# Attention with a quantised FFN on one core: v projected for two groups of heads at a time, and the start and the end of the kernel rearranged

## The chip, the cores and the metric

The kernel runs on one core of one Trainium2 chip. The core has engines that run side by side, each with its own queue of instructions in program order: PE (matrix products; PEld is its loading of the stationary operand), DVE (vector work), ACT (activation functions and copies), POOL (elementwise work) and SP (which here only starts DMAs). POOL and ACT can start DMAs too, from the same queues as their other work. The metric is the time on the device in microseconds (us); smaller is better.

## The reference

For x of shape (2, 1024, 512), with float32 data:

```python
def attn(x, w_q, w_k, w_v, w_o):                 # 32 heads of 16
    q, k, v = (proj(w) for w in (w_q, w_k, w_v)) # (2, 32, 1024, 16)
    scores = einsum('bhqd,bhkd->bhqk', q, k) / sqrt(16)
    out = einsum('bhqk,bhkd->bhqd', softmax(scores), v)
    return einsum('bse,oe->bso', merge_heads(out), w_o)

def bitlinear(x, w, scale):                      # ternary weights
    w_mean = mean(abs(w))
    return einsum('...i,oi->...o', x, clip(round(w / (w_mean + EPS)), -1, 1) * w_mean * scale)

def ffn(x, w_gate, w_up, w_down, ...):           # 512 -> 1376 -> 512
    xq = int4_quant(x)       # beta = mean|x| per token, values -8 to 7
    gate = square(relu(bitlinear(xq, w_gate, s_gate)))
    inter = int8_quant(bitlinear(xq, w_up, s_up) * gate)   # gamma = max|.| per token
    return bitlinear(inter, w_down, s_down)

x = x + attn(layernorm(x), ...)
x = x + ffn(layernorm(x), ...)
```

## The kernel before, in words

**Steps and slots.** The 32 heads are four groups g of eight; a group's heads lie in two sets s of four, 32 rows of the array each. The attention runs in 32 steps (batch b, half of the queries h, group g, set s), a step in 8 slots, one for each 128 keys. The loop over T runs the slots. In a slot PE forms scores for the exponentials (pse, line 515) and the scores of the next step for the row maxima (psm, line 475); ACT takes the exponentials (e, line 519), DVE the maxima (pm, line 485); PE then multiplies e with v (pso, line 545). The maxima are turned into rows by a small product (psn, line 498) and an ACT copy (mrow, line 502). All products of the attention are float32.

**Fillers.** Everything else is a generator whose pieces are laid between those products by the class `Fillers` while the program is built. It holds four lists: "proj", "norm", "ffn" and "back" (work without PE). A task may have a due slot; with fewer than `URGENT` (16) slots to go it comes first. A slot has a budget of PE time (`SHARE` or `MORE`). `WIDTH` says how many tasks of a list are looked at. A task that needs a PSUM bank yields ("take",), and ("give",) when done: it is given bank "o", or, if that is held, one of the score banks "s" if `fill.scores` allows (one in most of the loop's ends, three after the loop). `ensure(names)` runs fillers until the named tasks are done; it stands ahead of the loads of k (`load_k`, eight slots a step, five before the step) and of v (`load_v`, at slot 8n + 8). After the loop `turn()` goes through the tasks, one step of each in turn. The order of instructions on every engine is thus fixed when the program is built.

**The start.** `norm_inputs` loads four tiles of x by SP's queue (`xs`, line 280, four buffers), takes mean and variance on DVE, an inverse root by three Newton steps, normalises on DVE (line 294), transposes on PE (psx, line 302) and copies to xnT on ACT (line 303). Half 0 of the first batch runs straight away, then the first projections of k and q (psk and psq, line 390, `first_qk`); half 1, the rest of k and q for the first two steps and v of the first group are fillers. ACT's first instruction is the loading of its function table.

**Projections.** `project_qk` (lines 338 to 373) forms 128 x 512 of q or k in PSUM (line 351), copies it to `full` on ACT (line 359), casts to a rounded part `hi` and subtracts to get `lo` on POOL (lines 360, 361), and writes both to device memory by SP; `hi` and `lo` have two buffers each, `full` one. `project_v` (lines 410 to 437) runs for each (b, g, half): a 256 KB piece of weights wv by SP (line 333), 16 products of 128 x 128 by 128 columns into one bank (psv, line 418), two ACT copies into the one tile `vst` (line 430), which also holds columns of ones whose products give the softmax's sums, and two writes of 256 KB to vD by POOL's queue (line 432). `load_v` reads one (b, g, s) of 512 KB.

**Weights of the FFN.** A "back" task `weight_sums` (lines 627 to 646) loads 35 pieces of the three matrices by POOL's queue (tag raw, four buffers, three loads ahead) and sums absolute values on ACT (Abs into junk, line 640). Later `weight_quant` (lines 666 to 683) loads them again (raws), compares on POOL into `low` (line 677, two buffers) and makes the ternary fp8 weights on DVE.

**The end.** Work on the last step's sums: `normalise_last` copies the sums on ACT (den, line 589) and divides 128 columns (one tile of tokens) at a time, five DVE instructions each (lines 592 to 597, the result is OT). `output_proj` multiplies with w_o (psy, line 714; one product for each group, so four for a tile) and adds x on DVE (line 725), then statistics of the second normalisation (bn, root, beta; the sum of deviations `dev` on ACT). The last 512 tokens go in two calls of two tiles, (0, 1) and (2, 3). For each tile `ffn_input` normalises, clips and rounds (xn, xq, lines 768 to 774), transposes (psxq, line 780) and copies (xqT, ACT); `ffn_product` forms gate (pg) and up (pu) in three pieces of 512, 512 and 352 columns (line 801), with two ACT instructions on each gate piece (lines 811, 813) and on DVE the product of both (inter, line 823); `ffn_output` takes the maximum (gm, line 841), a few steps of one column (lines 843 to 847), scales (v, line 850), rounds on ACT (iq, line 853), transposes by eight and three products (psiq, line 863) with ACT copies (iqT), multiplies by the down weights in eleven products (py, line 880), adds (y, line 887) and writes out. Where a generator yields ("gap", n), it rests for n turns, and what other tasks issue meanwhile stands in between.

## Time and profile before

| what | value |
|---|---|
| median of 3 runs | 1307.87 us (1304.2 to 1317.62) |
| the profiled execution's own time | 1320.16 us |
| its span, first to last instruction | 1318.4 us |
| mean granted clock of PE | 0.965 |
| PE busy | 1209.3 us, 92% |
| DVE, ACT, POOL busy | 866.5, 712.1, 246.5 us |
| chain that ended last | PE 74%, DVE 11%, ACT 5%, issue 4%, DMA 4% |

The profile is one execution. Busy times add up over instructions; a clock of 1.00 is full speed of PE, 0.50 half of it. The chain that ended last goes back from the last instruction to whatever released it, step by step. A row of waits reads: engine, product and line, what it waited for, then the total of us, the number of times and the longest.

### The profile page before, as it was taken

The numbers are of one execution on the slowest core, as the hardware profiler recorded it, in microseconds if no ns is written. First come the engines' busy times: TensorE is split into PE (matmuls) and PEld (weight loads), VectorE is DVE, ScalarE is ACT, GpSimd is POOL, SyncE is SP. The second block draws the span as 40 slices with busy tenths as digits, with TensorE's granted clock in tenths as the row PEclk, the third lists the DMA queues.
The fourth block names the chain that finished last, engine by engine and source line by source line (L and its number), as shares of the span: only waits on it lengthen the run. The fifth ranks groups of instructions, "written<-read, shape, count | busy, mean of one in ns | idle before, by whom it ended". The sixth has DMA issues, their size and how long they took to land.

```text
span 1318.4 us, 22143 instructions
## 1 busy us (share of the span) xinstructions
PE 1209.3 (92%) x9082; PEld 541.6 (41%) x9082; DVE 866.5 (66%) x1203; ACT 712.1 (54%) x903; POOL 246.5 (19%) x279
## 2 busy tenths in 40 slices
PE   5768899999999999999999999999999999999566
PEld 2345444334445443444444444444433344443222
DVE  6521468778865667687776676877776867772634
ACT  1124655545655555665666556666665556666243
POOL 1034326455511100321101003110010111100000
PEclk9889999999999999999999999999999979999769
DMA  3056666555333431221213223211133110201000
GB/s 112 0 184 216 225 199 214 156 177 191 126 107 122 136 110 58 89 81 58 72 47 106 95 76 117 76 55 67 57 107 95 58 57 34 82 26 33 24 0 33
DMA packets 72334, 127.88 MB, mean 97 GB/s; under 512 B 9680, under 2 KB 30160, under 8 KB 72232
## 3 DMA queue, kind: packets, MB, share of 16 engines
q1 hardware_dynamic: 64360, 101.16, 23.8%
q0 software_dynamic: 7872, 25.30, 5.9%
q8 instruction: 71, 1.16, 0.4%
q14 instruction: 31, 0.25, 0.1%
HBM read 89.25 MB, written 37.19 MB: 96 GB/s over the span
## 4 chain that ended last, share of the span: by engine, by line
PE 74%; DVE 11%; ACT 5%; issue 4%; DMA 4%; POOL 2%; SPq 0%; ACTq 0%; DVEq 0%; POOLq 0%
PE pse L515 22%; PE pso L545 16%; PE psm L475 8%; PE psy L714 5%; PE psv L418 4%; DVE pm L485 4%; PE psq L351 3%; PE pu L801 3%; PE py L880 3%; PE psk L351 3%; DMA wv<-in_wvT 2%; PE pg L801 2%; ACT e L519 2%; PE psn L498 1%; PE psk L390 1%
## 5 line engine op out<-in xcount | busy, mean ns | idle before, releaser
L485 DVE TENSOR_REDUCE pm<-psm 128x2 f32<-128x1024 f32 x512 | 621.5, 1220 | 336.9 <-PE pse L515 236.8
L519 ACT ACTIVATE e<-pse 128x1024 f32<-128x1024 f32 x512 | 523.0, 1024 | 415.3 <-PE pse L515 315.4
L475 PE MATMUL psm<-kst,qst 32*128 32x512 f32 x2048 | 372.8, 448 | 13.4 <-ACT e L519 8.2
L515 PE MATMUL pse<-qst,kst 32*128 32x512 f32 x2048 | 371.7, 446 | 10.2 <-DVE pm L485 8.8
L515 PEld LDWEIGHTS pse<-qst,kst 32*128 32x128 f32 x2048 | 151.5, 185 | 325.0 <-issue 160.6
L545 PE MATMUL pso<-e,v 128*32 128x512 f32 x2048 | 277.5, 612 | 0.7 <-ACT po L554 0.4
L515 PE MATMUL pse<-mrow,onesr 2*128 2x512 f32 x1024 | 208.6, 406 | 0.0
L475 PEld LDWEIGHTS psm<-kst,qst 32*128 32x128 f32 x2048 | 152.5, 186 | 39.1 <-ACT e L519 27.9
L515 PEld LDWEIGHTS pse<-mrow,onesr 2*128 2x128 f32 x1024 | 95.3, 185 | 5.1 <-ACT mrow L502 0.2
L815 POOL TENSOR_TENSOR g<-g 128x512 f32<-128x512 f32 (+1 forms) x36 | 34.2, 951 | 315.6 <-ACT g L811 315.6
L418 PE MATMUL psv<-wv,xnT 128*128 128x128 f32 x512 | 70.7, 294 | 14.2 <-DMA wv<-in_wvT 12.0
L545 PEld LDWEIGHTS pso<-e,v 128*32 128x32 f32 x2048 | 40.7, 108 | 97.4 <-issue 94.5
L418 PEld LDWEIGHTS psv<-wv,xnT 128*128 128x128 f32 x512 | 64.0, 203 | 27.3 <-issue 19.7
L714 PE MATMUL psy<-wo,OT 128*128 128x512 f32 x128 | 66.7, 635 | 5.9 <-DVE OT L597 5.9
L351 PE MATMUL psq<-xnT,wq 128*128 128x512 f32 x120 | 60.9, 622 | 1.4 <-ACT full_k L359 1.4
L351 PE MATMUL psk<-xnT,wk 128*128 128x512 f32 x112 | 58.4, 640 | 1.5 <-ACT vst L430 1.5
L677 POOL TENSOR_SCALAR low<-raws,whalf 128x512 bf16<-128x512 f32 (+2 forms) x35 | 52.8, 1510 | 21.4 <-DMA raws<-in_wuT 8.5
L801 PEld LDWEIGHTS <-xqT 128*128 128x128 bf16 x384 | 33.1, 102 | 57.5 <-issue 38.0
L770 POOL TENSOR_SCALAR xn<-x,mv,a 128x512 f32<-128x512 f32 x12 | 24.9, 2073 | 166.8 <-DVE a L747 166.7
L801 PE MATMUL pg<-wg,xqT 128*128 128x512 fp8e4 (+1 forms) x192 | 49.9, 387 | 4.0 <-DVE inter L823 2.4
L801 PE MATMUL pu<-wu,xqT 128*128 128x512 fp8e4 (+1 forms) x192 | 47.6, 372 | 3.5 <-ACT g L811 2.5
L880 PE MATMUL py<-wd,iqT 128*128 128x512 fp8e4 (+1 forms) x176 | 45.1, 392 | 2.9 <-ACT g L811 1.7
(124 smaller groups left out, 841.6 us busy)
## 6 DMA issues: line engine op xcount, KB each, us to landing
v<-vD SPq DMA_DIRECT2D x32, 512.0 KB
kst<-kD SPq DMA_DIRECT2D x30, 512.0 KB
qst<-qD SPq DMA_DIRECT2D x60, 256.0 KB
vD<-vst POOLq DMA_DIRECT2D x32, 256.0 KB, 5.4
qD<-hi_q SPq DMA_DIRECT2D x30, 256.0 KB
qD<-lo_q SPq DMA_DIRECT2D x30, 256.0 KB
x<-in_x SPq DMA_DIRECT2D x16, 256.0 KB
wq<-in_wqT SPq DMA_DIRECT2D x16, 256.0 KB
```

The costliest lines, as they stand in the source:

```text
L351: nc.tensor.matmul(ps, w[:, c, :], xnT[b, h][:, c, :], start=(c == 0), stop=(c == KC - 1))
L418: nc.tensor.matmul(ps[:, i * P : (i + 1) * P], xnT[b, half][:, c, i * P : (i + 1) * P], w[:, c, :], start=(c == 0), stop=(c == KC - 1),)
L475: nc.tensor.matmul(ps[:, r % 2, :], qst[n][l][rows, t * P : (t + 1) * P], kst[n][rows, kh * QB : (kh + 1) * QB], start=(l == 0), stop=(l = ...
L485: nc.vector.tensor_reduce(pm[n][:, t, kh, 2 * j : 2 * j + 2], ps, AX.X, ALU.max, negate=True)
L515: nc.tensor.matmul(ps[:, r % 2, :], left, right, start=(l == 0), stop=(l == 2))
L519: nc.scalar.activation(e, ps, AF.Exp, scale=SCALE)
L545: nc.tensor.matmul(acc[n][32 * r : 32 * r + 32, :], vt[n][:, i, r, :], e[r // 2][:, r % 2, :], start=(i == 0), stop=(i == NT - 1),)
L677: nc.gpsimd.tensor_scalar(low, w, h[:rows, m, 1:2], None, ALU.is_lt)
L714: nc.tensor.matmul(ps, OT[b, h, g][:, i * P : (i + 1) * P], wo[g], start=(g == 0), stop=(g == NG - 1),)
L801: nc.tensor.matmul(ps, xT[:, c, :], w[:, c, n : n + size], start=(c == 0), stop=(c == KC - 1))
L815: nc.gpsimd.tensor_tensor(g2[j], g2[j], g2[j], ALU.mult)
L880: nc.tensor.matmul(py, iqT[:rows, c, :], wd[:rows, c, :], start=(c == 0), stop=(c == FC - 1))
```

## The change

v is projected for two groups at a time: one 512 KB piece of weights for an even g and the next (tag "wv", one buffer, held over both halves), products of 256 columns, in two pieces k of eight products for each half, and a single `vst` for the piece, which four ACT copies fill and one DMA of 512 KB writes. There are tasks for even g only; the second half follows the first. `load_v` reads its part of the pair's vD. In `project_qk` the tile `full` goes: ACT copies into `lo`, from which POOL casts `hi` and subtracts in place. Raw pieces have three buffers and two loads ahead, `low` one buffer. At the start the odd tiles of x are loaded by ACT's queue, and two of the four copies of the first half are made by DVE. `ensure` runs only projections that are due no later than the named ones, and `WIDTH` for them is 7 until first_1 is done. At the end `normalise_last` is a "back" task that divides tiles 2 and 3 after the first call of `output_proj` is done, with a mark for each tile; the second call comes after the first; POOL makes xn for tiles 1 to 3; `ffn_output` for the last 512 tokens has no gaps between its DVE steps, and cd comes after v. `feed` takes up tasks that still wait for an "out" or "quant" task.

```diff
...
         self.now = self.slot = 0
+        self.WIDTH = dict(self.WIDTH)
...
             self.held.append((task["kind"], self.now + 1))
+            task["kind"] = ""
...
         start = self.now
+        tasks = [t for t in self.tasks["proj"] if t["name"] in names]
+        due = max((t["due"] for t in tasks), default=0)
         while not set(names) <= self.done:
-            self.run(1e9)
+            self._back()
+            task = 1
+            while task:
+                task = next(
+                    (t for t in self._candidates() if (t["due"] <= due and t["list"] == "proj" or t["kind"]) and self._ready(t)),
+                    None,
+                )
+                if task:
+                    self._step(task)
+            self.now += 1
...
     mcols = [const.tile([P, TQ, P], F32R, name=f"mcols{k}") for k in range(2)]
-    vst = [const.tile([P, 2, 4, 4, 32], F32, name=f"vst{k}") for k in range(1)]
+    vst = const.tile([P, 2, 2, 2, 4, 32], F32, name="vst")
     for m in mcols:
         nc.gpsimd.memset(m.bitcast(F32), 0.0)
-    for v in vst:
+    for g in range(2):
         for s in range(2):
-            nc.gpsimd.memset(v[:, s, :, :, 16 * (1 - s) : 16 * (1 - s) + 16], 1.0)
+            nc.gpsimd.memset(vst[:, g, s, :, :, 16 * (1 - s) : 16 * (1 - s) + 16], 1.0)
...
             xs[t] = sb.tile([P, H], F32, tag="x", name=f"x_{b}_{t}", bufs=4)
-            nc.sync.dma_start(xs[t], x[b, t * P : (t + 1) * P, :])
+            (nc.scalar if fast and t % 2 else nc.sync).dma_start(xs[t], x[b, t * P : (t + 1) * P, :])
...
                 nc.tensor.transpose(ps[:, c * P : (c + 1) * P], xs[t][:, c * P : (c + 1) * P], ident)
-            nc.scalar.copy(
-                xnT[b, half][:, :, i * P : (i + 1) * P], ps.rearrange("p (c t) -> p c t", c=KC)
-            )
+            dst = xnT[b, half][:, :, i * P : (i + 1) * P]
+            if fast and half == 0 and i % 2:
+                nc.vector.tensor_copy(dst, ps.rearrange("p (c t) -> p c t", c=KC))
+            else:
+                nc.scalar.copy(dst, ps.rearrange("p (c t) -> p c t", c=KC))
...
     vD = {
-        (b, g, s): dram.tile([P, NT, P], F32, name=f"vD_{b}_{g}_{s}")
-        for b in range(B)
-        for g in range(NG)
-        for s in range(2)
+        (b, g): dram.tile([4, P, NT * P], F32, name=f"vD_{b}_{g}") for b in range(B) for g in range(0, NG, 2)
...
         hi = sb.tile([P, QB], F32R, tag="hi", name=f"hi_{name}", bufs=2)
-        lo = sb.tile([P, QB], F32R, tag="lo", name=f"lo_{name}", bufs=2)
-        full = sb.tile([P, QB], F32, tag="full", name=f"full_{name}", bufs=1)
-        nc.scalar.copy(full, ps)
-        nc.gpsimd.tensor_copy(hi, full)
-        nc.gpsimd.tensor_tensor(lo, full, hi.bitcast(F32), ALU.subtract)
+        lo = sb.tile([P, QB], F32, tag="lo", name=f"lo_{name}", bufs=2)
+        nc.scalar.copy(lo, ps)
+        nc.gpsimd.tensor_copy(hi, lo)
+        nc.gpsimd.tensor_tensor(lo, lo, hi.bitcast(F32), ALU.subtract)
...
-        for l, part in enumerate((hi, lo)):
+        for l, part in enumerate((hi.bitcast(F32), lo)):
...
-                    nc.sync.dma_start(dst[a], part.bitcast(F32))
+                    nc.sync.dma_start(dst[a], part)
             else:
                 dst = kD[b, g].rearrange("(e l d) q -> l e d q", l=2, d=16)[l]
-                nc.sync.dma_start(dst[:, :, h * QB : (h + 1) * QB], part.bitcast(F32))
+                nc.sync.dma_start(dst[:, :, h * QB : (h + 1) * QB], part)
...
     def project_v(b, g, half, have):
-        w = proj_weights(wvT, g, f"wv_{b}_{g}_{half}")
-        yield ("gap", 4)
+        if half:
+            w = wt.pop((b, g, "v"))
+        else:
+            w = wt[b, g, "v"] = sb.tile([P, KC, 2 * P], F32, tag="wv", name=f"wv_{b}_{g}")
+            nc.sync.dma_start(
+                w, wvT.rearrange("(c p) e -> p c e", p=P)[:, :, g * P : (g + 2) * P]
+            )
+            yield ("gap", 4)
         yield from done(have)
-        yield ("take",)
-        ps = spare(f"psv_{b}_{g}_{half}")
-        for i in range(4):
-            for c in range(KC):
-                nc.tensor.matmul(
-                    ps[:, i * P : (i + 1) * P],
-                    xnT[b, half][:, c, i * P : (i + 1) * P],
-                    w[:, c, :],
-                    start=(c == 0),
-                    stop=(c == KC - 1),
-                )
-            if i < 3:
-                yield ("pe", 940.0)
-        v = vst[0]
-        src = ps.rearrange("p (t r s d) -> p t r s d", t=4, r=4, s=2)
-        for s in range(2):
-            nc.scalar.copy(v[:, s, :, :, 16 * s : 16 * s + 16], src[:, :, :, s, :])
-        for s in range(2):
+        for k in range(2):
+            yield ("take",)
+            ps = spare(f"psv_{b}_{g}_{half}_{k}")
+            for i in range(2):
+                t = 2 * k + i
+                for c in range(KC):
+                    nc.tensor.matmul(
+                        ps[:, 2 * i * P : 2 * (i + 1) * P],
+                        xnT[b, half][:, c, t * P : (t + 1) * P],
+                        w[:, c, :],
+                        start=(c == 0),
+                        stop=(c == KC - 1),
+                    )
+                    if c == 1 or (c == KC - 1 and i == 0):
+                        yield ("pe", 860.0)
+            src = ps.rearrange("p (t g r s d) -> p g s t r d", t=2, g=2, r=4, s=2)
+            for j in range(2):
+                for s in range(2):
+                    nc.scalar.copy(vst[:, j, s, :, :, 16 * s : 16 * s + 16], src[:, j, s])
+            at = (4 * half + 2 * k) * P
             nc.gpsimd.dma_start(
-                vD[b, g, s][:, 4 * half : 4 * half + 4, :],
-                v[:, s].rearrange("p t r e -> p t (r e)"),
+                vD[b, g][:, :, at : at + 2 * P].rearrange("a p e -> p a e"),
+                vst.rearrange("p g s t r e -> p (g s) (t r e)"),
             )
-        yield ("give",)
-        yield ("pe", 940.0)
+            yield ("give",)
+            yield ("pe", 860.0)
+            yield ("gap", 1)
...
         vt[n] = sb.tile([P, NT, 4, 32], F32, tag="v", name=f"v_{n}", bufs=2)
-        nc.sync.dma_start(vt[n].rearrange("p t r e -> p (t r e)"), vD[b, g, s].rearrange("p t e -> p (t e)"))
+        nc.sync.dma_start(vt[n].rearrange("p t r e -> p (t r e)"), vD[b, g - g % 2][2 * (g % 2) + s])
...
         ot = sb.tile([P, QB], F32, tag="OT", name=f"OT_{b}_{h}_{g}", bufs=5)
+        OT[b, h, g] = ot
         for i in range(TQ):
+            if i == 2:
+                yield from done([f"out_{b}_{h}_0"])
...
-        OT[b, h, g] = ot
+            fill.done.add(f"tokens_{i}")
+            yield ("gap", 1)
...
         c, n, rows, cols = parts[i]
-        t = sb.tile([P, 512], F32, tag="raw", name=f"{name}{m}_{c}_{n}", bufs=4)
+        t = sb.tile([P, 512], F32, tag="raw", name=f"{name}{m}_{c}_{n}", bufs=3)
...
         raw = deque()
-        for k in range(len(todo) + 3):
+        for k in range(len(todo) + 2):
             if k < len(todo):
                 raw.append(load_raw(*todo[k], "raw"))
-            if k >= 3:
-                m, i = todo[k - 3]
+            if k >= 2:
+                m, i = todo[k - 2]
...
             w = raw.popleft()[:rows, :cols]
-            low = sb.tile([P, 512], BF16, tag="low", name=f"low{m}_{i}", bufs=2)[:rows, :cols]
+            low = sb.tile([P, 512], BF16, tag="low", name=f"low{m}_{i}", bufs=1)[:rows, :cols]
...
             yield ("gap", 1)
...
-    def output_proj(b, h, tiles):
+    def output_proj(b, h, tiles, last):
...
                     yield ("gap", 1)
+                if last and g == NG - 1:
+                    yield from done([f"tokens_{i}"])
...
         xn = sb.tile([P, H], F32, tag="tmp", name=f"xn2_{k}", bufs=3)
-        if last:
-            nc.vector.tensor_scalar(xn, xt, mean, a, ALU.subtract, ALU.mult)
-        else:
-            nc.gpsimd.tensor_scalar(xn, xt, mean, a, ALU.subtract, ALU.mult)
+        first = last and i == 0
+        (nc.vector if first else nc.gpsimd).tensor_scalar(xn, xt, mean, a, ALU.subtract, ALU.mult)
+        if not first:
...
         nc.vector.tensor_reduce(gm, v, AX.X, ALU.max, apply_absolute_value=True)
-        yield ("gap", 1)
+        if not last:
+            yield ("gap", 1)
...
-        nc.vector.tensor_scalar(cd, gm, 1.0 / 127.0, wscale[2], ALU.mult, ALU.mult)
-        yield ("gap", 1)
+        if not last:
+            nc.vector.tensor_scalar(cd, gm, 1.0 / 127.0, wscale[2], ALU.mult, ALU.mult)
+            yield ("gap", 1)
         nc.vector.tensor_scalar(v, v, f, MAGIC, ALU.mult, ALU.add)
-        yield ("gap", 1)
+        if last:
+            nc.vector.tensor_scalar(cd, gm, 1.0 / 127.0, wscale[2], ALU.mult, ALU.mult)
+        else:
+            yield ("gap", 1)
...
     early = [project_v(0, 0, half, ["ln_0_1"]) for half in range(2)]
-    for gen in early:
-        next(gen)
+    next(early[0])
...
     for half in range(2):
-        fill.add(f"v_0_0_{half}", early[half], due=3)
+        fill.add(f"v_0_0_{half}", early[half], ["v_0_0_0"] if half else [], due=3)
...
-                need = [f"{k}_{b - 1}_{g}_{half}" for g in range(NG) for k in "kqv"]
+                need = [f"{k}_{b - 1}_{g}_{half}" for g in range(NG) for k in "kqv" if k != "v" or g % 2 == 0]
...
                 fill.add(f"q_{b}_{g}_0", project_qk(b, g, 0, 0, have[:1]), due=due_k(n))
-                for half in range(2):
-                    fill.add(f"v_{b}_{g}_{half}", project_v(b, g, half, [have[half]]), due=due_v(n))
+                for half in range(2) if g % 2 == 0 else ():
+                    fill.add(
+                        f"v_{b}_{g}_{half}",
+                        project_v(b, g, half, [have[half]]),
+                        [f"v_{b}_{g}_0"] if half else [],
+                        due=due_v(n),
+                    )
...
                 name = f"out_{b}_{h}_{tiles[0]}"
-                ffns.append((name, output_proj(b, h, tiles), ready, 0))
+                ffns.append((name, output_proj(b, h, tiles, last), ready, 0))
+                ready = ready + [name]
...
     def feed():
...
-        while ffns and set(ffns[0][2]) <= fill.done | {ffns[0][2][0]}:
+        while ffns and all(a in fill.done or a[:3] in ("out", "qua") for a in ffns[0][2]):
...
         fill.slot = T
+        fill.WIDTH["proj"] = 4 if "first_1" in fill.done else 7
...
             b, h, g, s = steps[n]
-            fill.ensure(f"v_{b}_{g}_0", f"v_{b}_{g}_1")
+            fill.ensure(*(f"v_{b}_{g - g % 2}_{half}" for half in range(2)))
...
     fill.scores = 3
-    normalise_last(NSTEP - 1)
+    fill.add("norm_last", normalise_last(NSTEP - 1), (), "back")
...
```

## The prediction, made before the changed kernel ran

> **What bounds the kernel.** I read the slices first (PE's busy tenths, the granted clock):
>
> ```profile
> PE   5768899999999999999999999999999999999566
> ...
> PEclk9889999999999999999999999999999979999769
> ```
>
> PE is full from slice 6 to slice 36 and loose at both ends, where the clock falls too. The table by stage gives the amounts (microseconds of PE busy in each stretch, then the other engines, the clock, the DMA share):
>
> ```profile
> 0.00:66.00 66.00, 42.59 (x152) 20.64 (x153) 40.73 (x88) 9.48 (x15) 5.11 (x18) 0.90 0.20 56
> 66.00:165.00 99.00, 79.11 (x520) 46.95 (x518) 28.43 (x26) 47.45 (x102) 36.08 (x61) 0.93 0.64 208
> ...
> 345.00:1200.00 855.00, 837.85 (x6716) 364.32 (x6716) 611.30 (x772) 510.05 (x598) 114.56 (x106) 0.99 0.25 80
> ...
> 1220.00:1265.00 45.00, 24.43 (x76) 9.51 (x73) 23.92 (x84) 10.89 (x22) 0.00 (x0) 0.71 0.06 18
> 1265.00:1320.00 55.00, 35.41 (x176) 15.69 (x174) 25.48 (x49) 22.59 (x36) 0.00 (x0) 0.87 0.05 20
> ```
>
> The middle can lose only work of PE (98% busy); the ends hold 23, 20, 21 and 20 us of PE's idle time. The waits name their causes (total, times, longest):
>
> ```profile
> PE psx L302 <- DVE x L294: 16.1, 3, 11.8
> ...
> PE psxq L780 <- DVE xq L774: 13.2, 4, 10.3
> ...
> PE psv L418 <- DMA wv<-in_wvT: 12.0, 2, 8.7
> ...
> PE psy L714 <- DVE OT L597: 5.9, 2, 3.4
> ```
>
> The chain of waits between 60 and 125 us has the fetch of wv as its longest piece, because PE stands at v of the second group until it has landed:
>
> ```profile
> 77.83 18.57 DMA wv<-in_wvT
> ...
> 96.53 6.65 PE psv L418 x32
> ```
>
> **Products of v.** 256 products of 128 columns become 128 of 256. Eight old ones take 1.98 us in the loop; for 1024 columns in wide products the nearest row is psk's two 512-column products, 1.91. 32 such groups x 0.07 = 2.2 us, nearly all in the full stage: **-2**. Bounds: the first pair's 7.41 for 32 old products is 1.85 for eight (wide ones then +2); wide ones at 3.70 for four psk products, 1.85 for 1024 columns, against old ones at 2.0 give -4.7. ACT's copies become twice as many and half as long (the 128x256 copy is 0.37); in the loop ACT has room (510 of 855 us).
>
> **Start.** The odd x tiles go to ACT's queue. In the built order their third and fourth issue stand ahead of ACT's table load (1.28 us, done at 2.0 today, unseen) and of its first copies, and these two issues wait until psx_1 and psx_3 have freed the buffers. Psx_3 ends at about 15.5 today; with DVE's copies of tiles 1 and 3 (0.6 each) between its own steps, at 16.4. Then 1.28 + two copies of 0.58 put the first psk at 19.5 where it is 16.28: **+3.2**, between 1.5 (the table load overlaps something) and 4. It is carried to psv, 65.0 to 68.2.
>
> **First pair of v.** Before pse_0 there is now work for two groups: four pieces of 8 wide products at 1.85 to 1.91 per four, 3.8 each. The single vst makes each piece's copies wait until the previous piece's write on POOL's queue has landed (issue 0.54; writes of half its size land in 2.4 to 8.3 us, median 5.4, 2.6 in this stretch). Copies of about 1 us + 3.6 a round: first piece ready at 72, last copied at 86. ACT then has some raw Abs in its order ahead of mrow, so the first exp comes at 94 instead of 78.9, and 19 raw Abs (14 today) stand ahead of e_1_0. With three raw buffers, three Abs go per landing: 15 after the first exp are five rounds of landing (raw rows 3.5 to 8.9, raws median 6.0; I take 5) + 0.9, so e_1_0 is at 94 + 29.5 = 123.5 where it is 121.98: **+1.5**, at landings of 3.5 (its shortest) -6, at 6 +6.5. By then PE used to have done psk_2_0 and psq_2_0 (2 x 3.70), which are still to come: **+7.4**. The later wait for wv (12.0 - 8.7 = 3.3, and 0.9 of cold start) is gone: **-4.2**. The 8.7 us wait is gone too but sits inside the comparison at e_1_0: what is late next is ACT, whose exp stands in one queue behind the Abs. Head: **+4.7**, from -3 to +10.
>
> A rule against this part: the row is the 256 KB write's 2.4 to 8.3 us. The Trainium skill, "DMA: Bandwidth & Descriptors", puts about 2 us of fixed completion cost on every DMA. By it alone a round would be 3.5 us, not 4.6, and the first exp some 3 us sooner; the sum keeps the row.
>
> **Single buffers.** ACT's copy into lo now waits for the DMA from lo two projections ago, which POOL did before; POOL once waited 8.0 us so (hi_q), and behind ACT's copy stand exps, for which PE has two score banks. One low buffer puts POOL (1.57) and DVE (0.74) in series, off the path unless `quant` is due. From 0 to +8; most projections are further apart than the landings: **+1.5**. Raw's third buffer is counted above. The narrower `ensure` runs less at once; what it leaves undone is the +7.4.
>
> **Tail: the start.** The sums of tokens 0 and 1 are divided first. The last pso ends at 1221.54 today. Three psy products (0.85 each) are no longer ahead of it in PE's built order, and PE is full there (19.1 of 20 us before 1220), so it comes 2.6 sooner: **-2.6**; the times that follow are on today's scale. Den's copy now stands behind iq_0_3 (1.44) on ACT, so token 1 is divided at 1228.4 (two tokens of 2.16 after 1224), psy_1's last product has run by 1231, and from there to psxq_0 I take today's 11.8 (last psy 1240.2 to psxq 1252.04): 1243, 9 sooner. From there to the last psy PE has two psxq (0.40), pg_0, pg_512, pu_0 (1.02 each) and seven psy, 9.8, and 3 more for a cold start: 1255.6. Then x 0.7, inter 0.7, bn 0.8, root 2.3 on DVE, two dev on ACT (0.6 each), beta's small steps 1.3, gm 1.59, four small 0.85, v 0.94: iq_0 at 1266.5 where it is 1277.75, **-11**.
>
> **Tail: the cycle of a token.** Today iq_0 to iq_3 start at 1277.75, 1288.74, 1299.25, 1306.09: 11.0, 10.5 and 6.8 apart, 28.3 in all. Without the gaps the built order of DVE has y_k ahead of gm_(k+1), and PE's has psiq_(k+1) behind all of py_k. So one token is a chain with little beside it: psiq 0.72, pu_0 1.03, inter + clip + xq 1.55 (psiq's rest and pg_1024, 1.1, hide in it), psxq 0.40, pu_512 1.03, py 1.03, pu_1024 0.76, py 1.03, the next pg_0 1.03, py 0.81: 9.4; then y 0.75, gm 1.59, small 0.85, v 0.94, iq 1.44: 5.6; and some 0.6 between engines: 15.6. The last interval has no psxq and no next pg: 13.6. Together 44.8 against 28.3, **+16.5** at full clock. Xn moved to POOL costs nothing: it is done an interval ahead of clip. From iq_3 to the end today's 12.3 stay (its last py is at half clock already, 4.22 against 2.54 for py_2).
>
> While DVE and ACT do their 5.6, PE has pg_512 (1.0) and then idles some 4.6. What that does to the clock (its column stands before the last two) is in today's tail:
>
> ```profile
> 1225.00:1230.00 5.00, 2.43 (x3) 0.70 (x4) 4.73 (x17) 0.00 (x0) 0.00 (x0) 0.54 0.00 0
> ...
> 1255.00:1260.00 5.00, 3.63 (x9) 1.10 (x8) 0.00 (x0) 1.97 (x4) 0.00 (x0) 0.50 0.01 3
> ...
> 1280.00:1300.00 20.00, 15.89 (x87) 7.35 (x85) 12.49 (x25) 12.05 (x21) 0.00 (x0) 1.00 0.04 14
> ```
>
> After 3.4 us without a product (from 1221.5) PE ran at half clock; between 1252 and 1272 gaps of 0.55 to 0.85 kept it there, and it came back in the first stretch of some 4 us without one; gaps up to 1.4 at full clock (1280 to 1300) did not take it away. A gate or up group takes 1.87 at half clock, 1.02 at full. In the new cycle 4.6 is over 3.4, and the products after psiq stand close, so I let psiq, pu_0, psxq, pg_1024 and one more pu run at half: 3 a token, **+9**. Bounds: 0, if no clock is lost, and all 9.4 at half like 1252 to 1272, 8 a token, +24. The Trainium skill, "TensorE: Matmul & The Clock Gate", Part 1, says that half rate follows one idle window of about 3.4 us and ends after about as much busy time. By that rule alone each token would lose half of 3.4 us, +5 instead of +9, and the total be 4 lower; the rows of 1252 to 1272 are longer than it allows for gaps so short. Tail: -2.6 - 11 + 16.5 + 9 = **+12**, from +3 to +27.
>
> **Sum.** -2 + 4.7 + 1.5 + 12 = +16. The profiled run took 1320.16 (span 1318.4), 12.3 above the median 1307.87 and above all three timed runs; the terms are differences, so I add them to the median: **1324**.
>
> **Rivals.** (1) *The token cycle is set by DVE and ACT, not by PE's order*: today's last interval, 6.8, has no other token's work in between. If all three are so, the tail is -13.6 - 7.9 = -21.5 and the sum -17: 1291, faster. It decides at a mean spacing below 8.2. For: DVE is no longer broken by gaps. Against: y_k needs all of py_k, and gm_(k+1) stands behind y_k. (2) *No change that shows*: raws land in 3.5 (-7.5) and no clock is lost (-9): 1308. For: the shortest raw landing; against: 208 GB/s in that stage, the most of all. (3) *Half clock through the whole tail*, +24 for +9: 1339. For: 1252 to 1272; against: the new cycle's products stand closer. (4) *Width buys nothing* (7.41 for 32 old products): 2 to 4 up in any case, inside the others.
>
> **Chances.** A measurement of this kernel tells about 1% (13 us: 1294.8 and 1320.9). Forecast (1314 to 1334) 0.47, of which 0.37 above 1320.9; rival 2 0.21; rival 1 0.17; rival 3 0.15. Faster 0.17, same 0.10 + 0.21 = 0.31, slower 0.37 + 0.15 = 0.52. The range leaves out the lower two thirds of rival 1 and the upper half of rival 3: 1296 to 1341; the forecast's own is 1314 to 1334.
>
> **What would show it.** Right: first psk near 19.5; the first e near 94, with ACT waiting for vD at vst; no wait for wv at psv; psxq_0 10 us sooner after the last pso; iq starts 15 or more apart, PEclk near 0.6 in the tail. Wrong: iq starts under 11 apart, no Abs late in the head, or a stall in the middle (lo, low) that no row here holds.

## The result, and the profile after

The changed kernel takes 1365.4 us (median of 4 runs, 1353.7 to 1369.5), the kernel before 1308.1 in the same session (1304.2 to 1317.6): a ratio of 1.041, 95% interval 1.033 to 1.050. It is 57 us slower by the medians, 54 by the ratio; forecast was 16, with a range that ended at 1341. The side was right and the size was not.

The profiled execution took 1365.35, span 1363.6. The slices of its page:

```profile
PE   4775999899799999999999999999999989998664
...
PEclk9798899799899999999999999999999889998867
```

PE is no longer full from slice 6 on: there are dents at slices 8 and 11 (239 to 273 us and 341 to 375; slices counted from 1), where the kernel before had nines, and slice 4 fell from 8 to 5. The table by stage (PE, PEld, DVE, ACT, POOL busy, then clock, DMA share, GB/s):

```profile
0.00:66.00 66.00, 41.06 (x143) 19.49 (x144) 40.17 (x86) 7.64 (x12) 5.23 (x20) 0.90 0.19 60
66.00:165.00 99.00, 71.58 (x317) 33.97 (x317) 22.11 (x24) 37.97 (x95) 29.83 (x49) 0.84 0.55 163
165.00:345.00 180.00, 171.21 (x1224) 75.74 (x1222) 129.93 (x174) 95.53 (x127) 89.04 (x91) 0.96 0.58 179
...
1250.00:1300.00 50.00, 29.76 (x99) 13.20 (x100) 29.17 (x92) 16.04 (x28) 6.75 (x3) 0.80 0.05 16
1300.00:1365.00 65.00, 37.65 (x151) 17.01 (x149) 20.14 (x38) 18.36 (x31) 0.00 (x0) 0.71 0.04 17
```

Between 66 and 165 PE lies idle for 27 us where it was 20, and its clock fell from 0.93 to 0.84; the tail's clock went from 0.79 (1250 to 1320) to 0.71 (1300 to 1365). Busy time and shares say little more. What locates the loss is to follow one kind of instruction through both traces: ACT's 512 exponentials come in the same order in both, two a slot. The start of the n-th in each (us, read from the traces; "second before" is another profile of the unchanged kernel, from the first experiment):

| place | before | second before | after | after - before |
|---|---|---|---|---|
| first psk | 16.28 | 16.34 | 19.52 | +3.2 |
| first exponential | 78.90 | 74.45 | 96.57 | +17.7 |
| second slot's | 121.98 | 115.42 | 135.84 | +13.9 |
| step 1 | 159.65 | 154.61 | 173.78 | +14.1 |
| slot 23 | 229.33 | 222.87 | 246.63 | +17.3 |
| slot 26 | 242.29 | 235.80 | 271.57 | +29.3 |
| step 5 (slot 40) | 311.04 | 307.35 | 329.72 | +18.7 |
| step 6 (slot 48) | 344.34 | 340.56 | 374.07 | +29.7 |
| step 16 | 685.31 | 682.17 | 714.65 | +29.3 |
| last exponential | 1219.40 | 1215.15 | 1247.78 | +28.4 |
| last pso ends | 1221.54 | 1217.29 | 1249.90 | +28.4 |
| end of the span | 1318.4 | 1312.7 | 1363.6 | +45.2 |

So there are four places: the head (+14 by step 1), slots 23 to 26 (+12, of which 10 are made good by step 5, where in the kernel before PE waits 6.5 for DVE, between 250 and 312), slots 40 to 48 (+11, kept), and the tail (+16.8). From step 6 to the last exponential the two kernels run alike. The waits name what stands at the three first places. In the kernel before, ACT waited for raw pieces (junk is the output of Abs, the instruction that sums absolute values):

```profile
ACT junk L640 <- DMA raw<-in_wuT: 5.6, 4, 2.4
...
ACT junk L640 <- DMA raw<-in_wgT: 4.5, 4, 1.4
...
ACT junk L640 <- DMA raw<-in_wdT: 1.7, 1, 1.7
```

and after:

```profile
ACT junk L666 <- DMA raw<-in_wuT: 19.1, 7, 6.7
...
ACT junk L666 <- DMA raw<-in_wgT: 15.3, 3, 7.5
...
ACT vst L451 <- DMA vD<-vst: 8.4, 2, 4.3
...
PE psv L439 <- DMA wv<-in_wvT: 8.0, 1, 8.0
...
ACT lo_k L371 <- DMA qD<-lo_q: 7.6, 1, 7.6
...
ACT junk L666 <- DMA raw<-in_wdT: 7.2, 5, 2.7
```

ACT stands 41.6 us for raw pieces where it stood 11.8, and exponentials stand behind it; by how much they come later for it is a question for the experiments. Wv's fetch was the longest piece of the chain of waits here before. Between 60 and 200 us the chain now goes through landings of raw pieces, with one projection of q among them, whose copy on ACT and whose cast on POOL stand ahead of the next load:

```profile
94.75 9.92 DMA raw<-in_wgT
...
108.45 5.82 PE psq L364 x8
114.29 0.59 ACT lo_q L371
114.95 0.61 POOL hi_q L372
...
116.85 5.87 DMA raw<-in_wuT
...
123.84 3.48 DMA raw<-in_wuT
...
128.85 6.27 DMA raw<-in_wuT
...
136.22 8.06 DMA raw<-in_wuT
```

At slot 24 it is the copy into lo. ACT's timeline there (start, duration, and in brackets the idle time before it and what ended it):

```profile
249.44 0.58 ACT L524 CAST mrow<-psn 128x512 fp32r<-128x512 f32 x1
257.65 0.59 ACT L371 COPY lo_k<-psk 128x512 f32<-128x512 f32 x1 [7.63 <-DMA qD<-lo_q]
258.13 1.03 ACT L541 ACTIVATE e<-pse 128x1024 f32<-128x1024 f32 x1
```

A write of an older lo_q was issued by SP at 247.9 and took 9.7 to land; the exponential behind the copy is the one that PE's next maxima wait for (6.7 us). At slots 43 to 44 PE waits for the wv of batch 1, a fetch of 512 KB that was issued at 331.0 and landed 21.9 later (PE's timeline):

```profile
352.94 3.78 PE L439 MATMUL psv<-wv,xnT 128*128 128x256 f32 x8 [8.00 <-DMA wv<-in_wvT]
```

And the 3.78, for a group that takes 1.94 elsewhere, is half clock after the 8 us of idleness: from 352 to 357 the granted clock is 0.50.

### The profile page after: what moved, and what is told of

Same layout as the page of the kernel before. It is cut to its first block, busy times and chain, and to the rows that moved or that the text cites. A ratio compares the mean times of both kernels' runs of the same rounds, so it can differ in the third digit from the quotient of the medians.

```text
span 1363.6 us, 21611 instructions
## 1 busy us (share of the span) xinstructions
PE 1227.2 (90%) x8826; PEld 534.8 (39%) x8826; DVE 871.0 (64%) x1202; ACT 711.8 (52%) x933; POOL 250.0 (18%) x268
## 4 chain that ended last, share of the span: by engine, by line
PE 73%; DVE 10%; DMA 7%; ACT 5%; issue 3%; POOL 1%; SPq 1%; ACTq 0%; POOLq 0%; DVEq 0%
PE pse L537 22%; PE pso L567 15%; PE psm L497 8%; PE psy L742 5%; PE psv L439 4%; PE psq L364 4%; DVE pm L507 3%; PE pu L829 3%; PE py L913 3%; PE psk L364 2%; ACT e L541 2%; DMA raw<-in_wuT 2%; PE pg L829 2%; DMA wv<-in_wvT 2%; PE psk L402 1%
## 5 line engine op out<-in xcount | busy, mean ns | idle before, releaser
L497 PE MATMUL psm<-kst,qst 32*128 32x512 f32 x2048 | 376.1, 452 | 29.9 <-ACT e L541 24.3
L537 PE MATMUL pse<-mrow,onesr 2*128 2x512 f32 x1024 | 211.4, 411 | 3.4 <-ACT mrow L524 3.4
L439 PE MATMUL psv<-wv,xnT 128*128 128x256 f32 x256 | 65.4, 400 | 12.6 <-DMA wv<-in_wvT 8.0
L742 PE MATMUL psy<-wo,OT 128*128 128x512 f32 x128 | 71.3, 669 | 4.7 <-DVE OT L622 4.7
L364 PE MATMUL psq<-xnT,wq 128*128 128x512 f32 x120 | 63.7, 655 | 5.8 <-ACT lo_k L371 5.0
L364 PE MATMUL psk<-xnT,wk 128*128 128x512 f32 x112 | 61.3, 668 | 4.9 <-ACT lo_k L371 4.2
L797 POOL TENSOR_SCALAR xn<-x,mv,a 128x512 f32<-128x512 f32 x15 | 31.6, 2111 | 170.0 <-DVE a L775 169.9
L439 PEld LDWEIGHTS psv<-wv,xnT 128*128 128x128 f32 x256 | 47.1, 194 | 29.2 <-DMA wv<-in_wvT 8.4
L851 DVE TENSOR_TENSOR inter<-pu,g 128x512 f32<-128x512 f32 (+1 forms) x48 | 30.2, 630 | 33.5 <-PE pu L829 33.5
L829 PE MATMUL pu<-wu,xqT 128*128 128x512 fp8e4 (+1 forms) x192 | 50.8, 392 | 0.1
```

The costliest lines, as they stand in the source:

```text
L364: nc.tensor.matmul(ps, w[:, c, :], xnT[b, h][:, c, :], start=(c == 0), stop=(c == KC - 1))
L439: nc.tensor.matmul(ps[:, 2 * i * P : 2 * (i + 1) * P], xnT[b, half][:, c, t * P : (t + 1) * P], w[:, c, :], start=(c == 0), stop=(c == KC ...
L497: nc.tensor.matmul(ps[:, r % 2, :], qst[n][l][rows, t * P : (t + 1) * P], kst[n][rows, kh * QB : (kh + 1) * QB], start=(l == 0), stop=(l = ...
L537: nc.tensor.matmul(ps[:, r % 2, :], left, right, start=(l == 0), stop=(l == 2))
L742: nc.tensor.matmul(ps, OT[b, h, g][:, i * P : (i + 1) * P], wo[g], start=(g == 0), stop=(g == NG - 1),)
L829: nc.tensor.matmul(ps, xT[:, c, :], w[:, c, n : n + size], start=(c == 0), stop=(c == KC - 1))
```

## The experiments

The first experiments undo or ease one part each; the later ones take up what those left open. Only the gaps and the loads of x are put back as they were; lo, the sums and WIDTH are eased in another way, and no run has the fourth raw buffer back. Ratios are to the kernel before on the same chip, with 95% intervals; the changed kernel's is 1.041, and "off" means off its time, by the difference of the ratios.

**A second profile of the kernel before** (no edit).

> The kernel before, unchanged, for a second profile: the first profile took 1320.2 where the median of the timed runs is 1308. Theory A (the first profile holds a disturbance of some 12 us): this one takes 1304 to 1312, and the 12 us are missing at one place, the waits for wv being the likeliest (8.7 and 3.3 in the first profile). Theory B (being profiled costs time, or the kernel scatters all along its length): it takes 1318 or more, or 1308 with the difference spread over the whole loop.

1314.45, span 1312.7. The exponentials run 4.5 us earlier from the first one on and the tail is 1.5 shorter; after that the distance wanders between 3 and 6.5. So part of the first profile's 12 us was in the start, before any wv is waited for: psv starts at 59.8 instead of 65.0. The clock differs there: between 50 and 60 us it is 1.00 in the second profile and 0.83 in the first, for the same instructions. Neither theory was right; a difference of 5 us can come from one execution's clock in the head.

**The gaps put back.**

```diff
         nc.vector.tensor_reduce(gm, v, AX.X, ALU.max, apply_absolute_value=True)
-        if not last:
-            yield ("gap", 1)
+        yield ("gap", 1)
...
-        if not last:
-            nc.vector.tensor_scalar(cd, gm, 1.0 / 127.0, wscale[2], ALU.mult, ALU.mult)
-            yield ("gap", 1)
+        nc.vector.tensor_scalar(cd, gm, 1.0 / 127.0, wscale[2], ALU.mult, ALU.mult)
+        yield ("gap", 1)
         nc.vector.tensor_scalar(v, v, f, MAGIC, ALU.mult, ALU.add)
...
+        yield ("gap", 1)
```

> The changed kernel with the gaps of ffn_output for the last 512 tokens put back (cd before v again); the division of the sums in pairs, xn on POOL and everything else stay. In the changed kernel iq_0 to iq_3 start 17.2, 20.6 and 15.6 us apart (53.4), before 28.3. Theory A (without the gaps y_k stands ahead of gm_(k+1) and psiq_(k+1) behind py_k, so a token is one chain and PE falls to half clock): with the gaps the spacing is 10 to 12, 10 to 12 and 7 to 8, the tail after the last pso goes from 113.7 to 86 to 92, and the time falls by 22 to 27, to about 1340. Rival (the long cycle comes from the split division and the second pair's statistics between the tokens, or from a clock that is lost earlier): the spacing stays above 14 and the time falls by less than 8.

1331.0, ratio 1.013 (1.009 to 1.016): 2.8% or 37 us off. ACT's iq of the four tiles, in the changed kernel and then with the gaps:

```profile
1296.34 1.44 ACT L886 ACTIVATE iq<-inter,negmagic 128x1376 bf16<-128x1376 f32 x1 [3.33 <-DVE inter L880]
...
1313.58 1.44 ACT L886 ACTIVATE iq<-inter,negmagic 128x1376 bf16<-128x1376 f32 x1 [3.52 <-DVE inter L880]
...
1334.13 1.44 ACT L886 ACTIVATE iq<-inter,negmagic 128x1376 bf16<-128x1376 f32 x1 [3.53 <-DVE inter L880]
...
1349.72 1.44 ACT L886 ACTIVATE iq<-inter,negmagic 128x1376 bf16<-128x1376 f32 x1 [8.83 <-DVE inter L880]
```

```profile
1288.58 1.44 ACT L881 ACTIVATE iq<-inter,negmagic 128x1376 bf16<-128x1376 f32 x1
...
1301.15 1.43 ACT L881 ACTIVATE iq<-inter,negmagic 128x1376 bf16<-128x1376 f32 x1
...
1311.66 1.43 ACT L881 ACTIVATE iq<-inter,negmagic 128x1376 bf16<-128x1376 f32 x1
...
1318.49 1.44 ACT L881 ACTIVATE iq<-inter,negmagic 128x1376 bf16<-128x1376 f32 x1 [2.74 <-DVE inter L878]
```

17.2, 20.6, 15.6 become 12.6, 10.5, 6.8, and ACT is never idle ahead of the first three. The tail is 89.9 instead of 113.7: theory A. Of the 13 us more in the timed ratio the trace shows 10, and they are not of the edit's place: this execution was 4 us nearer from step 3 on, and 6 more came at steps 26 and 27 (see the last section).

**The sums at half the pace.** `yield ("gap", 1)` becomes `yield ("gap", 2)` in `weight_sums`.

> The changed kernel with the task of the absolute sums resting two turns instead of one between its pieces: 9 Abs instead of 19 stand ahead of the second slot's first exponential on ACT, the same 35 in all. In the changed kernel that exponential starts at 135.8, before at 122.0. Theory A (the head's loss is Abs that wait for their landings ahead of exponentials on ACT's queue): it starts at 112 to 122, step 1 starts some 10 to 15 sooner than the changed kernel's 173.8, and 8 to 14 us of it last to the end: 1352 to 1358. Rival (the loss is the single vst with its writes, and v of two groups ahead of the first scores): it starts within 5 of 135.8 and the time stays within 4.

1344.1, ratio 1.024 (1.019 to 1.028): 23 us off. The second slot's exponential starts at 124.7, 11 sooner but not the 14 to 24 expected, step 1 14.5 sooner, the end of the loop 13.5. Theory A holds in direction, and its rival (within 5 of 135.8) is out. The profiled execution, 1351.5, was the slowest of the four, so the 23 of the ratio can't be laid out place by place. Nor does this run say whether the third buffer or the pace makes the Abs late.

**Three buffers for lo.** `bufs=2` becomes `bufs=3` for the tag lo; `low` takes the tag junk, to make room.

> The changed kernel with three buffers for lo (room comes from junk and low sharing one buffer). In the changed kernel ACT's copy into lo_k stands 7.6 us at 250 until the DMA of an older lo has landed, with PE waiting 6.7 for the exponential behind it, and the distance to the kernel before grows from 17 to 29 us there (slots 46 to 52), to come back to 19 by step 5. Theory A (the single-buffer saving puts that DMA on ACT's path): the wait is gone, the distance stays below 20 through step 3, and the time falls by 6 to 12. Rival (the stall only takes up slack of what waits next, the fetch of wv at 345 or the quantisation): the wait is gone but the distance at step 6 is again 28 to 30 and the time changes by less than 4.

1353.2, ratio 1.031 (1.027 to 1.034): 14 off. The distance to the kernel before no longer jumps at slot 24 (14.1 there, 15.7 at slot 26) and the gain is kept to the end: 15.2 at step 6, 12.8 at the last pso. Nothing took the stall's place, against the rival; it was even a little more than the 6 to 12 of theory A.

**The projections looked at.** `fill.WIDTH["proj"] = 4` in the loop becomes 5.

> The changed kernel with WIDTH for projections 5 instead of 4 in the loop, so the task that fetches the next batch's wv is begun earlier: in the built order the fetch for batch 1 stands some nine DMAs of SP's queue sooner. In the changed kernel PE waits 8.0 us for it at 345, and the distance to the kernel before grows there by 11 us (from 19 at slot 80 to 30 at slot 96). Theory A (the one buffer and the late fetch of 512 KB cost what the old waits for wv cost): the wait falls below 2 and the time by 7 to 11. Rival (the transfer only changes places with loads of k, q and v, which are then late): the wait goes but another of at least 5 comes up between 320 and 380, and the time stays within 4.

1344.9, ratio 1.027 (1.022 to 1.032): 18 off. The wait for wv is gone, slot 44's exponential starts at 344.6 instead of 358.4 and the gain over the changed kernel is 12.5 at step 7: theory A up to there. At the last exponential it is 17.4; the last 5 come at steps 24 to 28, where the clock differs between executions (see the last section), and explain why 18 is above the 7 to 11 expected.

**x on SP's queue.**

```diff
-            (nc.scalar if fast and t % 2 else nc.sync).dma_start(xs[t], x[b, t * P : (t + 1) * P, :])
+            nc.sync.dma_start(xs[t], x[b, t * P : (t + 1) * P, :])
...
-            if fast and half == 0 and i % 2:
-                nc.vector.tensor_copy(dst, ps.rearrange("p (c t) -> p c t", c=KC))
-            else:
-                nc.scalar.copy(dst, ps.rearrange("p (c t) -> p c t", c=KC))
+            nc.scalar.copy(dst, ps.rearrange("p (c t) -> p c t", c=KC))
```

> The changed kernel with all tiles of x loaded by SP's queue and all copies of xnT on ACT, as before. Theory A (the fourth load on ACT's queue waits for psx_3 and holds up the table load and the copies): the first psk starts at 16.3 to 16.8 instead of 19.5, psv 3 sooner; of that 1 to 4 us reach the end. Rival (ACT's Abs and their landings set the first exponentials in any case): psk is 3 sooner, the second slot's exponential is within 1.5 of 135.8 and the time within 1.5.

1357.1, ratio 1.037 (1.032 to 1.042): 5.5 off, inside the changed kernel's interval. The first psk is at 16.34, 3.2 sooner as both said. Psv starts 8.6 sooner; the 5.4 beyond the 3.2 go with the clock between 40 and 60 us (0.78 and 0.83 against 1.00). The second slot's exponential is 8.5 sooner, where the rival had it within 1.5, and the last pso 5.0. That some of it lasts speaks for theory A; how much is not settled beside the clock.

**v for one group again**, in everything else the changed kernel: `project_v`, vst, vD and their tasks as before.

> The changed kernel with v projected for one group at a time again (products of 128 columns, one write of 256 KB for each set), and all else as changed, the three raw buffers, lo in place and the one low included. 17 Abs stand ahead of the second slot's first exponential instead of 19. Theory A (the head's loss is Abs waiting for landings with three buffers): the first exponential comes near 80 (v of one group, 7.4 instead of 14, and two rounds with the write instead of four), but the second slot's stays above 122; step 1 starts 3 to 8 sooner than the changed kernel's 173.8. Rival (the pair with its single vst is the head's loss): the second slot's exponential comes at 108 to 118 and step 1 starts 12 or more sooner. For the loop both: slots 128 to 384 take 546 in the changed kernel, 544 before; if wide products save their 2 us, this one takes 548, and if not, 544 to 546.

1345.0, ratio 1.030 (1.023 to 1.036): 15 off by the ratio. The first exponential is at 82.7, the second slot's at 125.5 and step 1 at 163.3, 10.5 sooner: between the two. The distance from the first to the second slot's exponential tells more: 43.1 before, 39.3 changed, 42.8 here. It did not grow with the change, although the raw pieces have a buffer less; the changed kernel is late at the second slot because it is late at the first, and 13.9 of the 17.7 at the first go when v is projected for one group. Exponentials 128 to 384 (slots 64 to 192; the expectation's numbers count exponentials) take 544.6, against 546.1 with wide products.

**Five undone together**: the edits of the gaps, the sums, lo, WIDTH and x in one kernel.

> The changed kernel with five things together: the gaps of the last tiles back, the sums resting two turns, three buffers for lo, WIDTH 5 and x on SP's queue. v for two groups, the division in pairs and the rest stay. If the losses add up, with 34, 21, 12, 9 and 3 off the changed kernel's 1365 it is near 1286, 2% faster than before. If they lie behind one another, as the lo stall and the later fetch of wv may, it is at 1300 to 1310, no faster than before.

1295.4, ratio 0.989 (0.985 to 0.993): faster than the kernel before. Singly the five make 37 + 23 + 14 + 18 + 5.5 = 98 us, together 68 (1.041 to 0.989): most of it adds up, some of it is the same time. The 68 is more than the change had cost, but the slower sums are no part of the change: the fifteenth experiment shows that the kernel before gains by them too.

**The clock kept in the tail.**

```diff
+        if last and i < 3:
+            yield ("take",)
+            pd = spare(f"warm_{k}")
+            for c in range(14):
+                nc.tensor.matmul(pd, iqT[:, 0, :], wd[:, c % 4, :], start=(c == 0), stop=(c == 13))
+            yield ("give",)
```

> The changed kernel with 14 products of 128 x 128 by 128 x 512 more after the down products of each of the last tiles 0 to 2, written to a PSUM bank that nobody reads: they fill 3.6 us at full clock of the stretch in which PE has nothing to do (DVE's y, gm, v and ACT's iq), and stand ahead of pg_512. Theory A (the cycle of a token is 15.6, 15.6, 13.6 at full clock, and half clock after the idle stretch adds the rest of the 17.2, 20.6, 15.6 measured): the clock stays at 1.00 in the tail, the three intervals fall to 44 to 47 in all from 53.4, and the tail from 113.7 to 104 to 107. Rival (the intervals are long for another reason, a bank or the order of DVE): the clock rises but the intervals stay above 50, or grow by what the additional products take.

1352.0, ratio 1.031 (1.028 to 1.034). The intervals are 17.1, 16.2, 13.7, 47.0 in all, the tail 105.9. The windows of the changed kernel around its second interval, and of this run from its second iq on (the clock stands before the last two columns):

```profile
1314.00:1320.00 6.00, 3.27 (x18) 1.82 (x19) 1.45 (x3) 3.13 (x4) 0.00 (x0) 0.52 0.00 0
1320.00:1326.00 6.00, 5.15 (x17) 2.10 (x16) 0.69 (x1) 1.98 (x5) 0.00 (x0) 0.50 0.00 0
1326.00:1332.00 6.00, 4.82 (x19) 1.93 (x17) 2.53 (x3) 1.23 (x2) 0.00 (x0) 0.84 0.06 24
```

```profile
1305.00:1311.00 6.00, 2.65 (x23) 1.56 (x24) 1.52 (x4) 4.39 (x8) 0.00 (x0) 1.00 0.00 0
1311.00:1317.00 6.00, 5.03 (x24) 2.34 (x24) 1.22 (x2) 1.53 (x4) 0.00 (x0) 1.00 0.01 3
1317.00:1323.00 6.00, 4.21 (x24) 1.90 (x23) 4.05 (x8) 2.46 (x3) 0.00 (x0) 1.00 0.12 44
```

More products, and a faster kernel: theory A. With the clock whole the second and third interval are 16.2 and 13.7, against the hand-made 15.6 and 13.6. The first, 17.1, has no such products ahead of it. So of the 23.5 us between the intervals without gaps (53.4) and with them (29.9) at least 6.4 are the clock, and up to 17 the order. The tail gives 7.8 of the 13 us off; the rest was gone before the last pso, which no part of this edit touches.

**The kernel before with the division in pairs alone** (`normalise_last`, its task, the order of the two calls and `feed` as changed).

> The kernel before with one part of the change alone: the sums of the last step divided in pairs, the second call of output_proj after the first, and what feed needs for it. All else, the gaps of ffn_output too, is as before. Theory A (the division in pairs is the part of the tail that gains, 90.0 against 96.9 and 95.4 after the last pso in the run with the gaps back): the tail is 88 to 91 and the time falls by 5 to 8, to 1303 to 1306 where before has 1311. Rival (that gain needs xn on POOL or comes from the clock of one execution): the tail stays at 94 or more and the time within 3.

1307.3, ratio 0.998 (0.996 to 1.0005). The tail is 95.4, as in the second profile of the kernel before. Psxq_0 comes 8 us sooner after the last pso (22.0 against 30.4), but iq_0 only 2 to 4. The last step, from its first to its last exponential, takes 19.8 where both profiles of the kernel before have 22.2. The rival: these 2.4 us are all that the division in pairs buys by itself, and the timed runs don't tell them from nothing.

**v for one group in the kernel with five undone.**

> The run with five things undone (1295, 0.989 of before), with v for one group at a time as well. Theory A (wide products save nothing in the loop, and the pair costs some 10 us ahead of the first exponential): the first exponential at 74 to 80 instead of 86, slots 128 to 384 within 2 of 545.7, and the time falls by 3 to 9, to 1286 to 1292. Rival (with the other waits gone the pair's weights, fetched once for two groups, are worth as much as its late start costs): within 2 of 1295 or above.

1310.8, ratio 0.999 (0.997 to 1.001): 13 slower than with five undone, against theory A and the seventh experiment. The first exponential is sooner (78.5), and up to step 16 the run is 5 ahead; it loses 5 in steps 16 to 20, 7 more up to the last pso, and 5.6 in the tail. In the last step it takes 22.7 where the run with five undone takes 19.8. This left the width open.

**The products alone made narrow**, with the fetch, pieces, writes and order of the five undone.

```diff
-                for c in range(KC):
-                    nc.tensor.matmul(
-                        ps[:, 2 * i * P : 2 * (i + 1) * P],
+                for a in range(2):
+                    for c in range(KC):
+                        nc.tensor.matmul(
+                            ps[:, (2 * i + a) * P : (2 * i + a + 1) * P],
...
-                        w[:, c, :],
+                            w[:, c, a * P : (a + 1) * P],
...
```

> The run with five things undone, with each product of v's 256 columns split into two of 128 and nothing else: the same fetches, pieces, copies, writes and the same order on all other engines. It measures the width alone. Theory A (a group of four wide products takes 1.94 where eight narrow ones take 1.98 to 2.05, 32 groups): 1.5 to 4 us slower. Rival 1 (the loop does not feel it): within 1.5 us. Rival 2 (width is what makes the run with five things undone 15 us faster than the one with v for one group): 8 us slower or more.

**Its partner on the same chip.**

> The run with five things undone again, beside the narrow one on the same chip, so that the two can be compared. If its 0.989 of before holds, 0.985 to 0.993 again, with the last down products at full clock (2.5 us) once more; if that was luck of the clock, nearer to 0.995.

1296.2, ratio 0.986 (0.984 to 0.989), and 1299.6, 0.989 (0.986 to 0.991). The groups of psv in the two (busy time, mean ns of a record, idle time ahead; each product leaves two records, so 512 are 256 products):

```profile
L438 PE MATMUL psv<-wv,xnT 128*128 128x128 f32 x512 | 65.4, 281 | 5.3 <-ACT vst L450 3.8 <-DVE kst L412 1.5
```

```profile
L437 PE MATMUL psv<-wv,xnT 128*128 128x256 f32 x256 | 63.6, 391 | 4.6 <-ACT vst L449 3.1 <-DVE kst L412 1.5
```

The wide products are busy 1.8 us less, and slots 64 to 192 take 545.2 narrow, 544.9 wide. The timed runs do not show it at all; the intervals overlap, with the narrow one's median the lower. The first rival: the width buys nothing that these runs can tell from nothing, at most some 1 us by the intervals. What v for one group lost in the run before this pair is then in what else it changed, the fetches, the writes and the order of the fillers, and in the tail's clock; which of them was not tried. The partner's last down products were at half clock this time (4.2), its tail 93.2 instead of 90.0, and its ratio held.

**Slower sums still**: three turns, in the kernel with five undone.

> The run with five things undone, with three turns instead of two between the pieces of the absolute sums. Theory A (Abs that wait for landings still stand ahead of the exponentials of steps 0 and 1): the second slot's first exponential 2 to 5 sooner than 115, 1 to 4 us off the time. Rival (at this pace the landings are hidden, and the later sums only delay the quantised weights): within 2 us or slower.

1289.7, ratio 0.983 (0.979 to 0.986): the fastest kernel of this study, 1.7% under the kernel before. The second slot's exponential is at 109.3, 8.8 sooner than in the run with two turns on this chip, and step 6 12 sooner. The profiled execution is the fastest of the six; by the ratios it is 8 us faster than that run and 5 faster than its narrow partner, so at least the 1 to 4 of theory A.

**The same edit alone in the kernel before.**

> The kernel before with one edit: three turns instead of one between the pieces of the absolute sums (four buffers and three loads ahead stay). 3 Abs instead of 14 stand ahead of the second slot's first exponential. Theory A (Abs that wait for landings ahead of exponentials cost the kernel before too, and the change only adds to an old cost): that exponential starts at 100 to 110 instead of 115 to 122, and the time falls by 6 to 15, to 0.988 to 0.995 of before. Rival (four buffers hide the landings; what costs is the change's three): the exponential moves by less than 4 and the time by less than 3; the wait for wv (8.7) is then what holds it.

1298.7, ratio 0.989 (0.984 to 0.994). The second slot's exponential stays at 117.8, held by a wait of 6.1 for wv as the rival says; but by step 6 the run is 17 to 21 ahead of the two profiles before, and no Abs waits for a raw piece any more. So the sums' hold on the exponentials was in the kernel before, too: theory A in the time, the rival at the second slot. With three turns in both, the kernel before is at 0.989 and the changed one with five undone at 0.983 (0.979 to 0.986): what is then left of the change is worth 9 us, with intervals that overlap a little, on two chips.

**Four turns.**

> The run with five things undone with four turns between the pieces of the sums (three gave 0.9825). Theory A: the second slot's first exponential is no longer behind any landing and comes at 105 to 109 or the same as with three turns (109.3), and the time is within 3 of that run's. Rival (each turn more buys more, or the later weights now stall the FFN): a difference of 5 or more, either way.

1298.1, ratio 0.989 (0.984 to 0.993). The second slot's exponential is 1.6 sooner still, but the run is 4 us behind that with three turns at step 8 and 9 at the last pso. By the ratios it is 8 us slower than three turns, but on another chip, with intervals that overlap a little, and the profile of three turns was the fastest of its six. Within 3 us, as theory A had it, is unlikely; that a fourth turn costs more than it brings is likelier than shown, and what would be late then was not traced.

## Why the prediction was wrong, step by step

**The start** was right: the first psk at 19.5 was forecast, 19.52 measured, and for the reason given, since ACT's queue is held by the loads of x until psx_3 is done and only then loads its table:

```profile
0.72 16.30 ACTq L294 DMA_DIRECT2D x<-in_x  x4
17.06 1.28 ACT L321 ACT_TABLE_LOAD   x1 [17.06 <-PE psx L316]
```

The first exponential was forecast at 94, and it was 96.6.

**The second slot's exponential, +1.5,** is the term of the head that was mis-sized: it is +13.9. I let five rounds of three Abs take 5.9 each, with a landing of 5, to reach 123.5; it took 39.3 from the first exponential to 135.84. Two things in the chain of the result section were not in that sum. The first landing takes 9.92, and all three of its round take 9.4 to 10.0 from the issue's end. And from 108.45 to 116.85 the next load stands behind the projection of q, its copy on ACT and its cast on POOL: a buffer comes free only when its Abs has run, ACT takes copies and Abs in order, and POOL issues the next load after what it has in its queue. I had nothing between the rounds. The middle landing is not at fault (median 5.2 after, 5.5 before, from 2.3 to 10.0 after). My range had landings of 6 for +6.5, and even that was short by 7.4. Next came +7.4 for two projections and -4.2 for the later wait for wv, together +3.2; the distance to the kernel before grew by 0.2 from the second slot to step 1 and by 3.4 up to slot 23, and no run separates the two terms. Nor does one separate what the lower clock of the head (0.84 for 0.93) costs by itself.

**"The later wait for wv is gone", -4.2**, holds for the head and is wrong for the kernel. One buffer for the pair moved the wait to the next batch: 8.0 us at slot 44, plus half clock after it, 11 us in all. I looked for the rows of the old waits and not for the next fetch in SP's queue, which the built order shows behind kst and qst.

**"Single buffers", +1.5 of 0 to +8.** The mechanism was named with its price: the wait for the DMA of an older lo would stand on ACT. (The row of the kernel before that I read as that wait on POOL, 8.0 us at hi_q, names the load of qst.) It came once, 7.6 us, and cost 12 between slots 23 and 26; without it the fourth experiment is 13 to 15 faster for good. I took the low end because "most projections are further apart than the landings"; but one that is not is enough. These three terms make most of what the loop lost: I had -2 + 4.7 + 1.5 - 2.6 = +1.6 for the last pso, and it is +28.4.

**Width, -2.** The twelfth and thirteenth runs can't tell it from 0. The rival that width buys nothing was right, and so was its place as a small one inside the others.

**The tail** was right: +14.5 after the last pso by my terms (-11 + 16.5 + 9) and +16.8 measured. Psxq_0 came 22.6 after it (forecast 21.5), iq_0 46.4 (45.0), and the three intervals 53.4 (44.8 + 9 = 53.8). The -2.6 ahead of the last pso came too: the last step went from 22.2 to 19.8. The rival that the cycle is set by DVE and ACT (spacing under 8.2) is out. So is "half clock through the whole tail" (+24). The clock's +9 is right in the sum and not in its parts: over the hand-made 15.6, 15.6 and 13.6 the three tokens lost 1.6, 5.0 and 2.0, and not 3 each. In the window table half clock lasts from 1314 to past 1326, in the second token; keeping the clock took 4.4 off the second interval (20.55 to 16.19) and 1.9 off the third (15.59 to 13.67). By the rule of the Trainium skill's page "TensorE: Matmul & The Clock Gate", Part 1, one window of about 3.4 us in each direction, a token would lose half of that, an estimate of 1.7. The third token agrees with it, and the second does not. One reading of mine was wrong: the gaps of up to 1.4 at full clock (1280 to 1300) are waits of the weight loads, and between products PE paused 0.97 there at most.

**The reference.** I added the terms to the median, because one profile stood 12 above it. The difference of the profiles is 45 to 51, that of the medians 57.

## What to carry to other kernels

A DMA that an instruction waits for costs what stands behind that instruction on its engine: before a buffer is taken away, ask on which queue its wait will stand, and price that at the longest landing in the trace and not at the middle one (7.6 us of waiting cost 12 here). Background work that runs on the engine of the critical path (Abs ahead of exponentials) should be paced so that its loads have landed when its turn comes; that one number was worth 1.1% in the kernel before. And "without gaps" is not faster where the gaps let the next tile's work in between: read the order that results, on every engine.

## What the hardware did that was not expected

The granted clock falls in the full stretch too, after a few microseconds in which DVE sets the pace, and not in every execution. In the kernel before PE was busy 2.94 of 5 us ahead of it, with no pause over 1.7 us, and then ran at half clock for over 10:

```profile
1046.00:1051.00 5.00, 2.94 (x28) 0.97 (x24) 4.52 (x18) 3.25 (x4) 0.00 (x0) 1.00 0.00 0
1051.00:1056.00 5.00, 4.73 (x26) 2.00 (x30) 4.90 (x9) 2.78 (x6) 0.00 (x0) 0.54 0.02 3
1056.00:1061.00 5.00, 4.32 (x28) 1.43 (x20) 3.52 (x10) 2.05 (x2) 0.00 (x0) 0.50 0.15 52
```

Step 26 took 40.9 and 40.2 us in the two profiles of the kernel before, 41.0 in the changed one (granted clock 0.90) and, with the same work, 37.6 with the gaps back (0.98). With v for one group it took 34.5 (1.00), but there DVE has 50 instructions in it where those two have 63, so not all of that is the clock. The last eleven down products took 2.54 in some runs and 4.2 to 4.9 in others, and the first psv started at 59.8 or 65.0 in the same kernel. Each is some 2 to 5 us, so a single pair of profiles can't tell a change of that size; the place where two traces part, and whether the clock parts there, can.
